# One hybrid layer stack on one core: own convolution taps ahead of the states, rotations one step later, the first memory layer in parts

## The chip, the cores and the metric

The kernel runs on one core of a Trainium2 chip. The metric is device time in microseconds (us) from the launch to the end on that core. The engines are named as in the profile: PE (TensorE, matmuls; PEld is its weight load), DVE (VectorE), ACT (ScalarE), POOL (GpSimd) and SP (SyncE, which issues most of the transfers). Each engine works through its own queue in order, and waits on semaphores for the others.

## The reference

The input x has 2 batches of 512 tokens with 512 channels, in float32. Six layers follow, each on a layer norm of x without weights:

```
x = x + 0.5 * ffn0(norm(x))      # int4 weights, 512 -> 1376 -> 512, silu(a) * b
x = x + ssm(norm(x))             # state-space layer, 128 heads of 64, 8 groups, state 128, chunks of 128
x = x + 0.5 * ffn0(norm(x))      # the same weights again
x = x + 0.5 * memory(norm(x))
x = x + attention(norm(x))       # 32 heads of 16, 8 key heads, rotary, causal
x = x + 0.5 * memory(norm(x))    # the same weights again
```

In the state-space layer a projection gives a gate, the rows hid, B and C, and dt. hid, B and C go through a causal convolution of four taps and a silu. Then each chunk has an inner part, (C B^T, times decays) times hid, and a part from the state that the chunks before it leave; the result is multiplied by silu(gate), normalised in groups of 1024 channels and projected back.

The memory layer computes, on a normed row h:

```
query  = h @ Wq.T                          # 64 wide
scores = (query @ Wr.T) @ (keys @ Wr.T).T / sqrt(48) + log_rel     # 128 slots
the 8 best slots by scores; weights w = softmax(query @ keys / 8 + log_rel) over them
out    = (w @ values) @ Wvd.T @ Wvu.T
u      = clip(0.5 * log1p(var h) / mean(log1p(var h)) + 2.5 * sigmoid(learned), 0, 5)
learned = gelu(h @ Wu1.T + bu1) @ Wu2.T
gate   = sigmoid(gate_w1 * clip((u - 0.5) / 1.5, 0, 1) + gate_bias), 0 below 0.05
return h + gate * out
```

The mean of log1p(var h) runs over all tokens of both batches.

## The kernel before

x stays on chip as eight tiles of 128 tokens by 512 channels (x[0] to x[7], batch b has the tiles 4b to 4b+3). `norm_parts` gives a norm in steps: `stats` (mean and variance, DVE), `root` (square root, ACT), `over` (reciprocal, DVE), `centre` (DVE; with a function `each` called on the normed tile) and `turn` (four transpositions on PE into a PSUM bank, hps, and a copy by ACT into hT). `start` is stats, root, reciprocal and centre in one.

Blocks written under `in_order` keep the order in which the code writes them on PE, DVE, ACT and POOL. Outside of them (memory setup, attention setup, nearly all of `memory`, and the second half of `end_last`) the framework's scheduler chooses the order: an instruction written earlier has priority, but one written later may go first when the earlier one isn't ready by its model. An `in_order` block's instructions may be interleaved with such free ones.

PSUM has eight banks, dealt out under names with a number of banks each; a matmul into a name waits until a bank of that name has been read. In the state-space stage they are tr 1, po 4, dd 1, mm 1, y 1; in the memory layers tr 2, mm 2, dd 2, y 2; in the attention pq 2 pairs, mx 2, av 1 and s 1.

The state-space stage is `period(n)`, n from 0 to 129: 128 steps (8 groups, in each both batches, in each 8 pairs of heads), and a pipeline in which step n is projected and convolved (`cur`), step n-1 (`p1`) makes its states and outputs, and step n-2 (`p2`) is projected back by `gather`. On PE a period has: the hid projection cp_h into dd (L881), a group's B or C projection into mm where it is due, the states st (L1074), the back projection po (L998), the outputs py in two halves (L1155, L1164), the gate projection pg into mm (L881), and transpositions of hid (L1208). On DVE it has, in order: hc, the gate's silu v (L904), two scans M (L972), the state recursion st (four operations, L1084), three own taps acc_h (`conv_taps`, L895), the taps of the B or C row, the products M with CB (L986), hid (L904), and yg (L1171, L1175). ACT has among others `first_tap` (acc, L890), the copy of the first state (L1079), the tanh th (L900), which closes `conv_taps`, and the exponentials of M.

`late` is the list of B and C rows of the group that comes next, each as three calls: `first` (first tap on ACT), `taps` (three taps on DVE, tanh on ACT) and `end` (silu on DVE). It holds one row in the sixth period of each eight (B) and in the seventh (C), and none in the others nor for the last group's second batch. Since cp_BT and cp_CT lie in mm, pg of the same period needs their taps to be done.

`memory` (L1255 on) is the first memory layer, written as one function for all tiles: norm, a second variance of each normed tile (`each`, L1264 to L1266), the mean of its logarithm (L1275 to L1285), then for each batch the gelu branch, the query, the route, scores and weights by tile (psc, sc, at, rest, top; L1338 to L1369), then one gate for all eight tiles (L1376 to L1400), and in an `in_order` block the additions to x with the attention's norm (L1410 to the end). The second memory layer is the class `Memory`, the same work in parts: `spread`, `learn`, `gelu`, `learned`, `query`, `route`, `score`, `weight`, `gate`, `add`. It takes the variance of the normed tile as variance times rstd times rstd, has one gate for each batch, and uses only the names dd, y and mm (and tr for turns). Its first batch is worked off within the attention, its second in `end_last`, after the attention.

In the attention, `attend` prepares batch 0 first and then runs 16 tiles (8 per batch) of four steps j. Each step has an `order` of maxima (mx), `weights` (PE: masks and scores w, L1774 and L1787; ACT: exponentials), `weigh` (av) and at j = 0 `normalise` (po in s); then come the `jobs` of that step; a tile ends with `turn_maxima` (pm in s, L1761; then mT on DVE). Batch 1's queries and keys are prepared by such jobs, in five units: `qk` in two halves (pqk in s; hi on ACT, lo and r on DVE, L1648 to L1672), `rotate` (prot in s, L1682; r on DVE; a POOL addition), `rotated` (rhi on ACT, rlo on POOL) and `spread_out` two or four times (pd in s, copied by ACT or DVE to q or k).

Of the kernel before, what the change touches and what calls it, by code (L numbers as in the profile page):

```python
# [10 lines left out]
F32 = mybir.dt.float32  # L11
# [7 lines left out]
P = 128  # L19
# [238 lines left out]
class Kernel:  # L258
# [135 lines left out]

    def norm(self, tag, each=None, gain=None):
        hT, start, turn = self.norm_parts(tag, each, gain)
        for t in range(NT):
            start(t)
            turn(t)
        return hT  # L400
# [602 lines left out]
    def period(self, n):  # L1003
# [29 lines left out]
        if cur is not None:  # L1033
# [21 lines left out]
            if n != 1:  # L1055
                conv = self.first_tap(p, cur.ct, f"h{cur.n}")
            if n == 0:
                th = self.conv_taps(*conv)
                self.group_bt(0, 0)
                self.turn(NT - 1, "po")  # L1060
                self.group_cb(0, 0, "po")
# [57 lines left out]
        if cur is not None:  # L1119
            if n > 0:  # L1120
                nc.scalar.activation(cur.M[1], cur.M[1], AF.Exp)
                self.setup_later(n, 1)
                th = self.conv_taps(*conv)
# [131 lines left out]
    def memory(self, n, then=None):  # L1255


        nc, m = self.nc, self.m
        with self.tc.tile_pool(name=f"mem{n}", bufs=1) as pool:
            mv2 = pool.tile([P, NT, 2], F32, name=f"mv2_{n}")  # L1260

            def each(t, h):
                st = pool.tile([P, 6], F32, tag="bn2", name=f"bn2_{n}{t}", bufs=3)
                nc.vector.bn_stats(out=st, in_=h)  # L1264
                nc.vector.bn_aggr(out=mv2[:, t, :], in_=st)
                nc.vector.scalar_tensor_tensor(  # L1266
                    out=self.x[t], in0=h, scalar=0.5, in1=self.x[t], op0=ALU.mult, op1=ALU.add
                )
                return h

            hT = self.norm(f"m{n}", each)


            lv = pool.tile([P, NT], F32, name=f"lv{n}")
            nc.scalar.activation(lv, mv2[:, :, 1], AF.Ln, bias=self.ones[:, 0:1])  # L1275
            tot = pool.tile([P, 1], F32, name=f"tot{n}")
            nc.vector.tensor_reduce(out=tot, in_=lv, axis=AX.X, op=ALU.add)
            pt = self.ps("tr", [P, 1], f"ptot{n}")
            nc.tensor.matmul(pt, lhsT=self.ones, rhs=tot, start=True, stop=True)
            nc.vector.tensor_scalar(  # L1280
                out=tot, in0=pt, scalar1=1.0 / (NB * S), scalar2=1e-6, op0=ALU.mult, op1=ALU.add
            )
            nc.vector.reciprocal(tot, tot)
            u = pool.tile([P, NT], F32, name=f"u{n}")
            nc.vector.tensor_scalar(  # L1285
                out=u, in0=lv, scalar1=tot, scalar2=0.5, op0=ALU.mult, op1=ALU.mult
            )

            sums = pool.tile([P, NT], F32, name=f"wsum{n}")
            learned = self.ps("y", [P, NT], f"learned{n}")  # L1290
            wT = []
            for b in range(NB):

                pz = self.ps("mm", [P, S], f"pz{n}_{b}")
                for k in range(KD):
                    nc.tensor.matmul(
                        pz, lhsT=m["m_wu1"][:, k, :], rhs=hT[b][:, k, :],
                        start=k == 0, stop=k == KD - 1,
                    )
                z = pool.tile([P, S], F32, tag="z", name=f"z{n}_{b}", bufs=2)  # L1300
                nc.scalar.activation(z, pz, AF.Identity, bias=m["m_cols"][:, 0:1])
                th = pool.tile([P, S], F32, tag="zt", name=f"zt{n}_{b}", bufs=2)
                nc.vector.tensor_tensor(out=th, in0=z, in1=z, op=ALU.mult)
                nc.vector.tensor_scalar(
                    out=th, in0=th, scalar1=0.044715, scalar2=1.0, op0=ALU.mult, op1=ALU.add
                )
                nc.vector.tensor_tensor(out=th, in0=th, in1=z, op=ALU.mult)
                nc.scalar.activation(th, th, AF.Tanh, scale=float(np.sqrt(2.0 / np.pi)))
                nc.vector.scalar_tensor_tensor(
                    out=th, in0=th, scalar=1.0, in1=z, op0=ALU.add, op1=ALU.mult  # L1310
                )
                for c in range(NC):
                    t = b * NC + c
                    nc.tensor.matmul(
                        learned[:, t : t + 1], lhsT=th[:, c * P : (c + 1) * P],
                        rhs=m["m_cols"][:, 1:2], start=True, stop=True,
                    )


                pq = self.ps("mm", [P, S], f"pq{n}_{b}")  # L1320
                for k in range(KD):
                    nc.tensor.matmul(
                        pq[:BOT], lhsT=m["m_wq"][:, k, :], rhs=hT[b][:, k, :],
                        start=k == 0, stop=k == KD - 1,
                    )
# [77 lines left out]
            with self.in_order():  # L1403
                if then is not None:
                    hT, _, turn = then()
                    stats, root, over, centre = self.norm_steps
# [610 lines left out]
```

## Time and profile before

| | us |
|---|---|
| median of 3 runs | 2785.98 |
| lowest and highest | 2782.41, 2788.01 |
| profiled execution, device time | 2794.43 |
| its span, first to last instruction | 2792.6 |
| PE busy | 2696.1 (97%) |
| DVE busy | 2029.1 (73%) |
| ACT busy | 1103.1 (40%) |
| POOL busy | 522.3 (19%) |
| first feed-forward layer, to about 283 | 283 |
| state-space stage, 283 to about 2125 | 1842 |
| second feed-forward layer, to about 2343 | 218 |
| first memory layer, to the first attention matmul at 2403.5 | 60.5 |
| attention, to about 2751 | 347.5 |
| rest of the second memory layer and the store | 41.6 |

The stage borders are read off the timeline. The mean granted clock of PE is 0.98 over the span: 1.00 in the state-space stage, 0.80 in the first memory layer, 0.93 and 0.90 in the attention's preparation and tiles, 0.74 in the last stretch. Durations of PE rows contain a modelled end, so neighbours overlap in the list by some 0.1 us. A float32 matmul shows as two passes of about 0.43 us for 512 columns at full clock.

### The profile page before, as it was taken

What the parts mean: (1) busy time and instruction counts of PE and PEld (TensorE: products, weight loads), DVE (VectorE), ACT (ScalarE), POOL (GpSimd) and SP (SyncE); (2) the same over time, 40 slices, a digit from 0 to 9 for tenths busy, and PEclk for the clock granted to TensorE, in tenths of its full rate; (3) what the DMA queues carried; (4) which work ended last, traced back from release to release, by engine and by line L of the source; (5) the groups of instructions that cost most, each with busy time, mean ns of one, the idle gap of its engine ahead of it and who ended that gap; (6) DMA issues with size and microseconds to landing.
All of it is one profiled execution on the core that took longest, in us unless ns stands there. A gap on an engine that the chain in (4) does not pass through costs nothing.

```text
span 2792.6 us, 33412 instructions
## 1 busy us (share of the span) xinstructions
PE 2696.1 (97%) x12208; PEld 1400.8 (50%) x12208; DVE 2029.1 (73%) x3627; ACT 1103.1 (40%) x2418; POOL 522.3 (19%) x344
## 2 busy tenths in 40 slices
PE   8999999999999999999999999999999999888997
PEld 3445555555555555555555555555555444445443
DVE  7846877888888788787787878878886443655555
ACT  2214443444444444344444434434443212344333
POOL 0001131323213222132322322223230000100000
PEclk9999999999999999999999999999999999889988
DMA  6623233223223323322322332232121010000000
GB/s 201 199 96 113 72 106 129 87 78 127 106 83 121 104 81 106 127 89 76 129 106 83 121 102 84 102 119 98 71 98 53 27 54 23 0 1 1 1 1 31
DMA packets 75620, 237.77 MB, mean 85 GB/s; under 512 B 9824, under 2 KB 10400, under 8 KB 58944
## 3 DMA queue, kind: packets, MB, share of 16 engines
q1 hardware_dynamic: 70416, 226.00, 23.6%
q10 hardware_dynamic: 4752, 8.65, 0.8%
q8 instruction: 97, 1.59, 0.2%
q0 software_dynamic: 288, 0.98, 0.1%
q14 instruction: 67, 0.55, 0.1%
HBM read 223.80 MB, written 11.80 MB: 84 GB/s over the span
## 4 chain that ended last, share of the span: by engine, by line
PE 84%; DVE 10%; ACT 4%; issue 1%; DMA 1%; POOL 0%; SPq 0%; ACTq 0%; DVEq 0%; POOLq 0%
PE pg L881 15%; PE po L998 14%; PE cp_h L881 14%; PE fo L667 5%; PE fmm L500 5%; PE py L1155 4%; PE st L1074 3%; PE fy L500 2%; DVE acc_h L895 2%; PE py L1164 2%; PE cp_BT L881 2%; PE cp_CT L881 2%; PE ht L1208 2%; PE w L1787 2%; PE fdd L500 1%
## 5 line engine op out<-in xcount | busy, mean ns | idle before, releaser
L881 PE MATMUL pg<-hT_s,wi 128*128 128x512 f32 x1024 | 472.5, 604 | 14.5 <-issue 6.9
L998 PE MATMUL po<-wo,yg 128*128 128x512 f32 x1024 | 460.7, 593 | 0.5 <-DVE yg L1175 0.5
L881 PE MATMUL cp_h<-hT_s,wi 128*128 128x512 f32 x1024 | 460.6, 592 | 0.0
L972 DVE TENSOR_TENSOR_SCAN M<-rows,later 128x512 f32<-128x512 f32 x256 | 458.4, 1829 | 0.0
L1182 POOL TENSOR_TENSOR ssum<-ssum,sq 128x512 f32<-128x512 f32 x112 | 142.3, 1270 | 1233.1 <-ACT sq L1181 1233.1
L881 PEld LDWEIGHTS pg<-hT_s,wi 128*128 128x128 f32 x1024 | 184.2, 189 | 221.7 <-issue 213.1
L895 DVE SCALAR_TENSOR_TENSOR acc_h<-cp_h,small,acc_h 128x511 f32<-128x511 f32 (+2 forms) x384 | 286.3, 745 | 9.0
L998 PEld LDWEIGHTS po<-wo,yg 128*128 128x128 f32 x1024 | 184.8, 190 | 184.4 <-issue 183.6
L881 PEld LDWEIGHTS cp_h<-hT_s,wi 128*128 128x128 f32 x1024 | 184.6, 190 | 183.6 <-issue 183.6
L988 POOL TENSOR_TENSOR Cs<-CT,rows 128x768 f32<-128x768 f32 x128 | 252.1, 1970 | 17.4 <-PE py L1164 15.7
L1084 DVE SCALAR_TENSOR_TENSOR st<-st,whole,st 128x64 f32<-128x64 f32 x512 | 108.8, 274 | 125.5 <-ACT st L1079 125.5
L900 ACT ACTIVATE th_h<-acc_h 128x512 f32<-128x512 f32 x128 | 80.5, 629 | 292.2 <-DVE acc_h L895 286.5
L1027 ACT ACTIVATE hd<-ht,end 128x64 f32<-128x64 f32 x768 | 171.1, 324 | 35.6 <-DVE hc L1019 35.5
L1181 ACT ACTIVATE sq<-yg 128x512 f32<-128x512 f32 x112 | 70.6, 630 | 287.1 <-DVE yg L1175 287.1
L986 DVE TENSOR_TENSOR M<-M,CB 128x512 f32<-128x512 f32 x256 | 164.6, 684 | 0.1
L977 ACT ACTIVATE M<-M 128x512 f32<-128x512 f32 x128 | 80.6, 630 | 199.1 <-DVE M L972 199.1
L1751 DVE CUSTOM_DVE_ANT_0 j<-s,future 128x384 f32<-128x384 f32 (+3 forms) x256 | 112.8, 487 | 53.4 <-PE s L1741 53.0
L1019 DVE TENSOR_TENSOR hc<-ht,dt 128x512 f32<-128x512 f32 x128 | 88.1, 689 | 85.6 <-PE ht L1208 85.6
L1155 PEld LDWEIGHTS py<-M,hc 128*64 128x64 f32 x2048 | 109.4, 136 | 68.2 <-issue 64.7
L1155 PE MATMUL py<-M,hc 128*64 128x128 f32 x2048 | 140.5, 279 | 1.1 <-DVE M L986 1.1
L1074 PEld LDWEIGHTS st<-hd,Btok 128*128 128x128 f32 x768 | 104.0, 191 | 70.2 <-issue 41.6
L904 DVE SCALAR_TENSOR_TENSOR v<-v,pg 128x512 f32<-128x512 f32 x128 | 87.5, 684 | 50.0 <-ACT v L1015 47.7
(386 smaller groups left out, 3780.7 us busy)
## 6 DMA issues: line engine op xcount, KB each, us to landing
rows<-rows SPq DMA_DIRECT2D x128, 1024.0 KB, 4.7
wi<-in_w_in_dram SPq DMA_DIRECT2D x144, 256.0 KB, 3.4
wo<-in_w_out_dram SPq DMA_DIRECT2D x64, 256.0 KB, 3.2
keep<-w ACTq DMA_DIRECT2D x33, 256.0 KB, 3.5
wk<-keep SPq DMA_DIRECT2D x33, 256.0 KB, 2.7
wi<-in_q_dram SPq DMA_DIRECT2D x44, 128.0 KB, 3.1
sc<-in_s_dram SPq DMA_DIRECT2D x44, 128.0 KB, 3.3
wi<-in_q_dram SPq DMA_DIRECT2D x11, 256.0 KB, 3.5
```

Of the source, the lines that this page charges most:

```text
L500: nc.tensor.matmul(dst, lhsT=w[:, k, :], rhs=x[:, k, :], start=start and k == 0, stop=stop and k == 1, skip_group_check=True,)
L667: nc.tensor.matmul(po, lhsT=act[ht][:, b, c * P : (c + 1) * P], rhs=w2[ht], start=ht == 0, stop=ht == NHT - 1,)
L881: self.nc.tensor.matmul(p, lhsT=wt[:, k, :], rhs=self.hT[b][:, k, :], start=k == 0, stop=k == KD - 1)
L895: self.nc.vector.scalar_tensor_tensor(out=acc[:, s:], in0=p[:, : S - s], scalar=w[:, 3 - s : 4 - s], in1=acc[:, s:], op0=ALU.mult, op1=ALU ...
L972: self.nc.vector.tensor_tensor_scan(out=m, data0=rows[:, i, 0, :], data1=self.later, initial=0.0, op0=ALU.add, op1=ALU.mult,)
L986: self.nc.vector.tensor_tensor(out=m, in0=m, in1=sh["CB"], op=ALU.mult)
L988: self.nc.gpsimd.tensor_tensor(out=cur.Cs, in0=sh["CT"][:, P:].unsqueeze(1).to_broadcast([P, 2, S - P]), in1=cur.rows[:, :, 1, P:], op=ALU ...
L998: self.nc.tensor.matmul(self.po[c], lhsT=p2.yg[:, c * P : (c + 1) * P], rhs=self.wo[p2.ct], start=p2.q == 0, stop=p2.q == PAIRS - 1,)
L1027: nc.scalar.mul(hd[:, c, ch], p1.pt[:, c, ch], self.dec["dt_end"][:, b * NC + c, h0 + i : h0 + i + 1],)
L1074: nc.tensor.matmul(pst[:, c, :], lhsT=self.sh[p1.g, p1.b]["Btok"][:, c, :], rhs=hd[:, c, :], start=True, stop=True,)
L1155: nc.tensor.matmul(py[ch, cs], lhsT=hc[:, c, ch], rhs=p1.M[i].rearrange("p (c t) -> p c t", c=NC)[:, c, :], start=c == 0, stop=c == 0, ski ...
L1182: nc.gpsimd.tensor_tensor(out=self.ssum, in0=self.ssum, in1=sq, op=ALU.add)
```

## The change

Four things are edited.

- `period`: where `late` is not empty, the own `conv_taps` (three taps on DVE, tanh on ACT) is written right after the own first tap, ahead of the states; in the other periods it stays where it was.
- `attend`: for each of batch 1's five units, `rotate` moves from step 3 of tile t to step 0 of tile t+1, `rotated` from step 0 to step 1, and each `spread_out` one step on.
- `memory`: the long function is replaced by an object of the class `Memory` with number 0. Its parts are called in the order learn, gelu, query, route, learned, then score and weight for each tile, then gate, batch by batch; the closing block is unchanged but for `m.add(t)`. So the second variance of each tile goes, the gate is made per batch, sc and rest have one buffer instead of two, and the bank names are those of `Memory`.
- `end_last`: for batch 1 of the second memory layer, query and route are written first, then learn, then the scores and weights, and gelu, learned and gate(0) after them.

The function `norm`, which only the old `memory` called, goes too.

```diff
@@ period
             if n != 1:
                 conv = self.first_tap(p, cur.ct, f"h{cur.n}")
+            if n == 0 or late:
+
+                th = self.conv_taps(*conv)
             if n == 0:
-                th = self.conv_taps(*conv)
                 self.group_bt(0, 0)
...
             if n > 0:
                 nc.scalar.activation(cur.M[1], cur.M[1], AF.Exp)
                 self.setup_later(n, 1)
-                th = self.conv_taps(*conv)
+                if not late:
+                    th = self.conv_taps(*conv)
             for one in late:
                 one[1]()
@@ memory
-    def memory(self, n, then=None):
...
+    def memory(self, then):
+        with self.tc.tile_pool(name="mem0", bufs=1) as pool:
+            m = Memory(
+                self, 0, pool, lambda tag, name: pool.tile([P, S], F32, tag=tag, name=name, bufs=2)
+            )
+            for t in range(NT):
+                m.start(t)
+                m.turn(t)
+            m.spread()
             for b in range(NB):
...
+                m.learn(b)
+                m.gelu(b)
+                m.query(b)
+                m.route(b)
+                m.learned(b)
                 for c in range(NC):
...
+                    m.score(b, c)
+                    m.weight(b, c)
+                m.gate(b)
             with self.in_order():
...
+                hT, _, turn = then()
+                stats, root, over, centre = self.norm_steps
                 for t in range(NT):
...
+                    m.add(t)
                     stats(t)
                     if t % NC == NC - 1:
                         root(t + 1 - NC, t + 1)
@@ end_last
         m.spread()
-        m.learn(1)
-        m.gelu(1)
         m.query(1)
         m.route(1)
-        m.learned(1)
-        m.gate(0)
+        m.learn(1)
         for c in range(NC):
             m.score(1, c)
             m.weight(1, c)
+        m.gelu(1)
+        m.learned(1)
+        m.gate(0)
@@ attend
             job(t, 1, self.qk, 1, u, 0)
             job(t, 2, self.qk, 1, u, 1)
-            job(t, 3, self.rotate, 1, u)
-            job(t + 1, 0, self.rotated, 1, u)
+            job(t + 1, 0, self.rotate, 1, u)
+            job(t + 1, 1, self.rotated, 1, u)
             for i in range(4 if u == 4 else 2):
-                n, j = divmod(4 * t + 5 + i, 4)
+                n, j = divmod(4 * t + 6 + i, 4)
                 job(n, j, self.spread_out, 1, u, i, "s")
```

## The prediction

> **What bounds the kernel now.** I read the page's head and clock row first, then the list of waits for the state-space stage, then the timeline where those waits fall, and last the timelines of the attention and memory stages.
>
> ```profile
> span 2792.6 us, 33412 instructions
> ...
> PE 2696.1 (97%) x12208; PEld 1400.8 (50%) x12208; DVE 2029.1 (73%) x3627; ACT 1103.1 (40%) x2418; POOL 522.3 (19%) x344
> ...
> PEclk9999999999999999999999999999999999889988
> ```
> ```profile
> PE pg L881 <- issue: 6.9, 14, 0.7
> PE pg L881 <- DVE acc_BT L895: 5.1, 7, 0.7
> PE pg L881 <- DVE acc_CT L895: 2.4, 7, 0.3
> ```
>
> TensorE is busy 97% of the span, so only what makes PE wait, or work at a lower clock, counts. The second fence is the whole of PE's notable waiting between 270 and 2125 us (the next entry is 1.6 us): 28 waits ahead of the gate projection pg, 14.4 us. They lie in the 30 "late" periods, in which a B or C row of the next group is convolved too. An ordinary period repeats every 13.29 us, a late one every 17.4 us (pg starts 437.52, 454.97, 472.40).
>
> ```profile
> 449.51 0.86 DVE L1084 SCALAR_TENSOR_TENSOR st<-st,whole,st 128x64 f32<-128x64 f32 x4 [4.11 <-ACT st L1079]
> ...
> 450.29 2.31 DVE L895 SCALAR_TENSOR_TENSOR acc_h<-cp_h,small,acc_h 128x511 f32<-128x511 f32 x3
> ...
> 452.51 2.31 DVE L895 SCALAR_TENSOR_TENSOR acc_BT<-cp_BT,small,acc_BT 128x511 f32<-128x511 f32 x3
> ...
> 454.97 3.67 PE L881 MATMUL pg<-hT_s,wi 128*128 128x512 f32 x8 [0.73 <-DVE acc_BT L895]
> ```
>
> This is the late B period in the timeline (start, duration, engine, line, output<-input, and in brackets the idle time and its releaser). VectorE (DVE) stands idle for 4.11 us until the state copy on ScalarE (ACT) frees st; only then come the own taps (acc_h) and the B taps (acc_BT), and pg, which needs the bank that acc_BT reads, starts 0.73 us late. In the C period the wait is 0.34 us.
>
> ```profile
> 2488.67 0.47 PE L1714 MATMUL pd<-rlo,spread 128*128 128x512 f32 x1 [0.47 <-DVE O L1824]
> ...
> 2500.55 0.47 PE L1682 MATMUL prot<-hi,spread 128*128 128x512 f32 x1 [0.81 <-DVE r L1672]
> ...
> 2502.04 0.66 PE L1761 MATMUL pm<-masks,top 128*128 128x128 f32 x4 [0.78 <-DVE r L1685]
> ...
> 2506.79 0.27 PE L1774 MATMUL w<-mask 128*128 128x128 bf16 x2 [0.64 <-ACT w L1793]
> ```
>
> In the attention stage the rotation matmul (prot) waits 0.81 us for the bank that VectorE still reads, and the transposition of maxima (pm) behind it 0.78 us. The first and last lines show what stands at a first step (j = 0): 0.47 us behind the normalisation, 0.64 us for the exponentials.
>
> ```profile
> 2388.59 0.75 DVE L1413 SCALAR_TENSOR_TENSOR x<-pmo,gate,x 128x512 f32<-128x512 f32 x1
> ...
> 2394.94 0.72 DVE L1413 SCALAR_TENSOR_TENSOR x<-pmo,gate,x 128x512 f32<-128x512 f32 x1
> ...
> 2403.46 1.02 PE L1659 MATMUL pqk<-hT_a,a_wqk 128*128 128x512 f32 x2
> ```
> ```profile
> 2774.52 0.28 DVE L189 SCALAR_TENSOR_TENSOR sc<-psc,m_rel 128x128 f32<-128x128 f32 x1
> ...
> 2784.28 1.41 DVE L253 SCALAR_TENSOR_TENSOR x<-pmo,gate,x 128x512 f32<-128x512 f32 x2
> ```
> ```profile
> 2343.00:2403.50 60.50, 50.01 (x168) 25.01 (x168) 40.26 (x130) 22.73 (x48) 0.00 (x0) 0.80 0.07 26
> ...
> 2360.00:2374.00 14.00, 14.00 (x38) 6.92 (x38) 6.09 (x31) 2.62 (x8) 0.00 (x0) 0.63 0.00 0
> ```
>
> The three fences above: first the end of the first memory layer, with the first addition to x, which needs the whole gate, at 2388.59, the fifth at 2394.94, the first attention matmul at 2403.46; then the kernel's end, from the first score row to the last additions; then, per stretch, length, busy time and count of PE, weight loads, DVE, ACT and POOL, and the granted clock: the layer takes 60.5 us at 0.80.
>
> **A, own taps ahead of the states.** Nothing is added; in 30 late periods three taps (2.31 us) and a tanh (0.63 us) move ahead of the state recursion. At 442 us the scans end by 445.40 (449.51 - 4.11) and the first tap on ACT at 445.84, so taps run to 448.2 and the tanh to 448.8, before the st copy is ready (449.22). Then st (0.86) and acc_BT end at 452.7 instead of 454.82; PE would come to pg at 454.24, so the 0.73 us goes, with 1.5 us to spare. In the C period the own tanh ends at 467.2, where the st copy ran at 466.65: the copy slips 0.6 us, st ends at 468.4, acc_CT at 470.7, and PE comes to pg at 472.06: 0.34 us goes, 1.3 us to spare. Behind the waiting tanh on ACT are the st copy, the B or C row's first tap and the second exponential; the next users are py's second half (at 471.2, st done 468.4) and times_c, both later. What is late next is nothing but PE. Sum: -14.4 us, from -12 (half of the C waits kept) to -15.4 (30 times the mean 0.51).
>
> **B, rotations one step later.** Five units. Each leaves step 3: prot's wait stays, since pm needs the same single bank (0.81), but prot's two passes (about 0.65, 2500.55 to the last pass) and pm's own wait (0.78) go: -1.43 x 5 = -7.2. At the next step 0, prot must wait until the normalisation is read (0.47) and takes 0.65, but the masks behind it wait 0.64 + 0.15 today: +0.3 in four units, +0.9 in the first, where no such wait stands: +2.1. The spreads end at step 3 now, so pm or the value projection waits for the q copy; such a wait is 0.7: three times, +2.1. The last k spread lands ahead of the first q projection in the same bank: +0.7. In the last unit two such waits move one step and remain. The rope multiply (0.69 on VectorE) falls where it is idle 0.72 for maxima; POOL's addition and subtraction (1.27 each) keep a whole step of 4 us. Sum -2.3; taken -2.2, from -5 (new waits covered by those for the exponentials) to +3 (all seven new waits and no cover).
>
> **C, first memory layer in parts.** Removed: 8 statistics rows (5.5 us for 8, 0.69 each) and 8 aggregates (0.17) on VectorE, replaced by two small multiplies (0.16). VectorE paces the last rows from 2346.15 on; the hT copies end at 2353.9 and would end near 2352: -1.9. With a gate for each batch, batch 0's gate depends on scores done by 2375.2, and VectorE waits for batch 1's queries until 2380.9. So four additions with their statistics (2388.59 to 2394.94) can lie there: -6.35. The attention's first norm still stands behind the fifth addition, which needs batch 1's gate, so its 8.5 us tail stays. Added: a second set of nine gate operations (about 0.2 each, 1.8 us, hidden in the same gap; +1.8 if not), one-buffer scores (1.83 us a block at the kernel's end against 1.65 here: +0.7 a batch), and a square root for batch 0 that can now fall between exponentials: two more table loads of 1.28 and 0.30, of which ACT's gaps hide about half, +1.3. Sum -6.3, from -11 (the second batch's queries come earlier too) to +5 (the rival below).
>
> A rule speaks against this last part. The trace's load is 1.28 us and the next activation follows within 0.01 us of it (2354.83 to 2356.12). The Trainium skill, page "ScalarE: Activation LUTs", section "What ACT_TABLE_LOAD costs", gives about 1283 ns plus a drain of about 1380 ns, 2.66 us for each switch. By that the two switches would cost 5.3 us in place of 2.6 and C would be near -5; the duration in the trace is used.
>
> **D, queries first at the end.** The query chain today starts behind pmz: pmq runs 2766.17 to 2769.8, scores start at 2774.52. Put first, pmq starts at 2760.76 in pmz's place at the same low clock; the route follows near 2768, and scores, behind pmz's rest on PE, start near 2771.5: -3. But gelu's four VectorE operations (0.69 + 0.43 + 0.69 + 0.69 = 2.5 us), which hide under the query chain today, now share VectorE with the scores, and two additions (0.75 each) made in its gaps today may follow: +2.5 to +4. Sum +0.5, from -2.5 (scores run ahead of pmz's rest) to +4 (gelu, its tanh and the gate wholly behind the scores).
>
> **Sum.** -14.4 - 2.2 - 6.3 + 0.5 = -22.4 us. The profiled execution took 2794.43 us (span 2792.6 and 1.8 around it), so 2772.0; it is 0.3% above the median of the runs, 2785.98, from which the forecast is 2763.6, say 2764.
>
> **Rivals.**
> 1. The memory layer gains nothing. Scores, transposed weights and projections now share two "dd" banks, so batch 1's projections hold the bank that batch 0's transposed weights need; PE is full between 2360 and 2374 at a clock of 0.63. Serial blocks, at most 3.6 us each (1.83, exponential 0.6, transposition and copy 0.7, hand-overs 0.5), make 29 us for eight against about 20 now, +9, and eat the -6.35. Then 2785.98 - 14.4 - 2.2 + 0.5 and up to +5: 2770 to 2775.
> 2. The wait ahead of pg only changes its releaser. If something else than the taps held that bank, A is worth 0: 2786 - 8 = 2778. For it, half of the waits (6.9 us) name no releaser; against it, they come at the same places and lengths (0.69, 0.30) with the taps ending just before.
> 3. Slower: the own tanh holds the st copy. On ACT's queue it now stands ahead of the st copy and of the next row's first tap. If the own taps start 2.2 us or more later than I place them, as with late scans, pg waits more than today. Each further microsecond costs 30. At 2.4 us pg would wait 1.15 instead of 0.48: +20 - 8 = +12, 2798. Against it: the scans show no wait for their rows.
> 4. More is gained: queries of batch 1 move up too and D gives its -2.5: near 2756.
>
> The granted clock is a fifth unknown, without a sign: the attention's first two tiles ran at 0.57 and 0.72, and the first took 20.4 us where later ones take 17.2, so one dip more or less is about 3 us. The Trainium skill, page "TensorE: Matmul & The Clock Gate", section "Part 1: The HAM clock gate", says that an idle window of about 3.4 us halves the clock. That agrees with 0.64 from 2389 to 2403, where PE waits 3.65 us; it gives no sign either.
>
> **How the numbers follow.** Likeliest 0.62; rival 1 0.17; rival 2 0.08; rival 3 0.07; rival 4 0.06. The likeliest's own range is 2756 to 2772; with the bounds of C and D and rivals 1, 2 and 4 it is 2751 to 2780. A measurement can tell about 0.2%, 5.6 us. The likeliest, rivals 1 and 4 and most of rival 2 are faster: 0.87; part of rival 2, 0.05, within; rival 3 and a poor sum of B, C and D, 0.08, slower.
>
> **What would show it.** A: no wait ahead of pg, late periods of 16.7 and 17.1 us, th_h ending before the B or C taps; else A is wrong. B: prot at step 0, pm in even tiles with one wait, not two. C: four additions to x before batch 1's scores end, the first attention matmul some 50 to 55 us after 2343, table loads between exponentials. D: scores starting before gelu's multiplies, and an end that moves less than 3 us. The prediction is wrong if pg still waits, or if the memory layer is as long as before.

## The result, and the profile after

The changed kernel takes 2763.39 us (median of four, 2761.28 to 2766.91), the kernel before 2786.02 us beside it (2782.41 to 2788.01). The ratio is 0.9918, with a 95% interval from 0.9891 to 0.9945: 22.8 us less, where 22.4 were forecast. The total is right; the terms of the sum are not. By the profiles, two gave more than forecast, one gave nothing, and one took a little.

The profiled execution of after took 2761.28 us (span 2759.5), that of before 2794.43 (span 2792.6). The head and the clock row of the page of after:

```profile
span 2759.5 us, 33377 instructions
...
PE 2680.9 (97%) x12208; PEld 1394.8 (51%) x12208; DVE 2000.5 (72%) x3622; ACT 1108.9 (40%) x2428; POOL 522.5 (19%) x344
...
PEclk9999999999999999999999999999999999889997
```

PE is as full as before; the last slices of the clock are a little higher. By stage, each length read between rows of PE's timeline:

| stage (us) | before | after | difference |
|---|---|---|---|
| start to the first pg | 250.9 | 249.1 | -1.8 |
| state-space stage and the feed-forward layer behind it | 2092.1 | 2072.9 | -19.2 |
| first memory layer (p_vd to the first pqk) | 60.5 | 61.4 | +0.9 |
| attention (first pqk to the first row of the last output projection, pao) | 343.5 | 327.5 | -16.0 |
| end (from there) | 45.7 | 48.6 | +2.9 |

Not all of the first two differences belongs to the change. The first pg starts at 248.4 to 250.9 us in the profiles of kernels without A, and the first period of the state-space stage takes 20.3 to 23.2 us with A and without it. From the second pg to p_vd it is 2069.7 us before and 2052.6 after, 17.1 us less.

**A.** The notable waits of PE between 270 and 2112 us, in the list of waits of after (total, times, longest us), begin:

```profile
PE st L1069 <- ACT hd L1020: 0.9, 2, 0.5
PE pd_whole L791 <- DVE CB L949: 0.8, 1, 0.8
```

No wait ahead of pg is left. The late B period in the timeline of after:

```profile
440.56 2.32 DVE L888 SCALAR_TENSOR_TENSOR acc_h<-cp_h,small,acc_h 128x511 f32<-128x511 f32 x3 [0.48 <-ACT acc_h L883]
442.97 0.63 ACT L893 ACTIVATE th_h<-acc_h 128x512 f32<-128x512 f32 x1 [2.44 <-DVE acc_h L888]
...
444.15 0.85 DVE L1079 SCALAR_TENSOR_TENSOR st<-st,whole,st 128x64 f32<-128x64 f32 x4 [1.27 <-ACT st L1074]
444.93 2.31 DVE L888 SCALAR_TENSOR_TENSOR acc_BT<-cp_BT,small,acc_BT 128x511 f32<-128x511 f32 x3
...
448.86 3.70 PE L874 MATMUL pg<-hT_s,wi 128*128 128x512 f32 x8
```

The own taps and their tanh (th_h) fill VectorE's gap, the states and the B taps follow, acc_BT ends at 447.24, 1.6 us ahead of pg (1.5 forecast), and pg has no bracket: it did not wait. The late periods are now 16.72 us (B) and 17.05 us (C), from 17.5 for B and 17.4 for C.

**B.** In the timeline of the attention stage after:

```profile
2476.47 0.66 PE L1618 MATMUL pm<-masks,top 128*128 128x128 f32 x4 [0.72 <-DVE r L1529]
...
2480.63 0.47 PE L1539 MATMUL prot<-hi,spread 128*128 128x512 f32 x1 [0.47 <-DVE O L1681]
...
2494.72 0.66 PE L1618 MATMUL pm<-masks,top 128*128 128x128 f32 x4 [0.68 <-ACT V L1583]
```

The rotation stands at a first step behind the normalisation (0.47), pm of an even tile (2476.47) has one wait in place of two, and the next pm (2494.72) waits for a copy: as forecast.

**C.** The additions to x on VectorE after, and the first attention matmul on PE, in the timeline:

```profile
2351.97 0.75 DVE L253 SCALAR_TENSOR_TENSOR x<-pmo,gate,x 128x512 f32<-128x512 f32 x1
2353.58 0.72 DVE L253 SCALAR_TENSOR_TENSOR x<-pmo,gate,x 128x512 f32<-128x512 f32 x1
2361.79 0.75 DVE L253 SCALAR_TENSOR_TENSOR x<-pmo,gate,x 128x512 f32<-128x512 f32 x1 [0.65 <-PE pmo L248]
2364.72 0.75 DVE L253 SCALAR_TENSOR_TENSOR x<-pmo,gate,x 128x512 f32<-128x512 f32 x1 [0.30 <-PE pmo L248]
2374.93 0.75 DVE L253 SCALAR_TENSOR_TENSOR x<-pmo,gate,x 128x512 f32<-128x512 f32 x1
...
2383.41 1.02 PE L1516 MATMUL pqk<-hT_a,a_wqk 128*128 128x512 f32 x2
```

Four additions did move ahead of the second batch's scores, and only the fifth stands behind them. The layer is no shorter all the same. Why can be read where it is cut at the first score, at the last transposed weight and at the attention's first transposition. The middle two pieces, as stretches (length, busy time and count of PE, weight loads, VectorE, ScalarE and POOL, granted clock, DMA share and rate), first before, then after:

```profile
2361.99:2388.17 26.18, 22.09 (x69) 10.71 (x68) 16.03 (x76) 7.36 (x23) 0.00 (x0) 0.76 0.00 0
2388.17:2397.40 9.23, 4.83 (x8) 1.63 (x8) 8.78 (x20) 2.17 (x3) 0.00 (x0) 0.68 0.00 0
```
```profile
2340.67:2374.47 33.80, 27.51 (x77) 12.41 (x76) 24.36 (x97) 12.04 (x34) 0.00 (x0) 0.71 0.00 0
2374.47:2377.33 2.86, 0.47 (x2) 0.18 (x2) 2.61 (x8) 0.27 (x1) 0.00 (x0) 0.50 0.00 0
```

Behind the last weight 6.37 us are gone (9.23 to 2.86; 6.35 forecast). Between the first score and the last weight 7.62 us came in. What came in between is on PE of after:

```profile
2351.58 0.47 PE L213 MATMUL pmw<-masks,at 128*128 128x128 f32 x1 [0.75 <-ACT at L203]
2351.84 5.27 PE L126 MATMUL pmz<-hT_m,m_wu 128*128 128x512 f32 x8
2357.04 3.65 PE L162 MATMUL pmq<-hT_m,m_wq 128*64 128x512 f32 x8
```

The second batch's projections (pmz, pmq) start only when the first batch's fourth transposed weight (pmw) is through. That is 29.8 us after p_vd, where before the first chunk of that projection stood just ahead of the first batch's scores, 17.8 us after p_vd, and the rest among them. ScalarE's two forecast table loads are there too:

```profile
2364.03 1.28 ACT L352 ACT_TABLE_LOAD   x1
2367.18 0.30 ACT L352 ACTIVATE rstd_a<-mv_a,eps 128x4 f32<-128x4 f32 x1 [1.86 <-DVE mv_a L349]
2368.12 1.28 ACT L203 ACT_TABLE_LOAD   x1 [0.64 <-DVE top L202]
```

Ahead of the first score a third load has moved: the one for the logarithm of the variances. It ran behind the last copy of hT before; now it runs between the first copy and the second, and PE waits for that copy. ScalarE's row of before, then the rows of ScalarE and PE after:

```profile
2354.83 1.28 ACT L1275 ACT_TABLE_LOAD   x1
```
```profile
2325.86 1.28 ACT L108 ACT_TABLE_LOAD   x1
...
2327.98 1.14 PE L381 MATMUL hps_m<-masks,h_m 128*128 128x128 f32 x8 [1.43 <-ACT hT_m L387]
```

**D.** The end in VectorE's timeline after:

```profile
2737.63 0.29 DVE L189 SCALAR_TENSOR_TENSOR sc<-psc,m_rel 128x128 f32<-128x128 f32 x1 [4.50 <-PE psc L183]
...
2738.23 0.67 DVE L136 TENSOR_TENSOR mt<-mz 128x512 f32<-128x512 f32 x1
...
2747.04 0.17 DVE L221 TENSOR_SCALAR gate<-gate 128x4 f32<-128x4 f32 x1 [2.52 <-ACT gate L156]
...
2755.71 0.75 DVE L253 SCALAR_TENSOR_TENSOR x<-pmo,gate,x 128x512 f32<-128x512 f32 x1 [0.95 <-PE pmo L248]
```

The scores start 21.9 us ahead of the end (18.1 before), and gelu's multiplies lie among them. Then VectorE stands for 2.52 us, with half a score block in hand, because a gate operation stands ahead in its order and waits for the learned gate's tanh.

### The profile page after: what moved, and what is told of

It reads as the page before. It is cut to its first block, busy times and chain, and to the rows that moved or that the text cites. A ratio compares the mean times of both kernels' runs of the same rounds, so it can differ in the third digit from the quotient of the medians.

```text
span 2759.5 us, 33377 instructions
## 1 busy us (share of the span) xinstructions
PE 2680.9 (97%) x12208; PEld 1394.8 (51%) x12208; DVE 2000.5 (72%) x3622; ACT 1108.9 (40%) x2428; POOL 522.5 (19%) x344
## 3 DMA queue, kind: packets, MB, share of 16 engines
q1 hardware_dynamic: 70416, 226.00, 23.9%
## 4 chain that ended last, share of the span: by engine, by line
PE 86%; DVE 8%; ACT 4%; issue 1%; POOL 0%; DMA 0%; SPq 0%; ACTq 0%; DVEq 0%; POOLq 0%
PE po L991 15%; PE pg L874 14%; PE cp_h L874 13%; PE fo L660 5%; PE fmm L493 5%; PE py L1151 4%; PE st L1069 3%; PE py L1160 3%; PE fy L493 2%; PE cp_CT L874 2%; PE cp_BT L874 2%; PE ht L1204 2%; DVE acc_h L888 1%; PE w L1644 1%; PE fdd L493 1%
## 5 line engine op out<-in xcount | busy, mean ns | idle before, releaser
L965 DVE TENSOR_TENSOR_SCAN M<-rows,later 128x512 f32<-128x512 f32 x256 | 431.2, 1723 | 0.0
L979 DVE TENSOR_TENSOR M<-M,CB 128x512 f32<-128x512 f32 x256 | 165.9, 684 | 12.5 <-ACT M L1116 12.3
```

Of the source, the lines that this page charges most:

```text
L965: self.nc.vector.tensor_tensor_scan(out=m, data0=rows[:, i, 0, :], data1=self.later, initial=0.0, op0=ALU.add, op1=ALU.mult,)
L979: self.nc.vector.tensor_tensor(out=m, in0=m, in1=sh["CB"], op=ALU.mult)
```

## The experiments

**The four parts alone, each on the kernel before.** The edits are the four pieces of the diff shown above; the third (the memory layer) is the changed kernel with the other three undone:

```diff
+            if n == 0 or late:
+                th = self.conv_taps(*conv)
             if n == 0:
-                th = self.conv_taps(*conv)
...
-                th = self.conv_taps(*conv)
+                if not late:
+                    th = self.conv_taps(*conv)
```


> Own taps ahead of the states alone, on the kernel before. Theory 1 (the late periods give what the trace of the changed kernel shows, 16.0 us in 28 of them and 1.5 in the first two): about 17 us faster, 2769, ratio 0.994, late periods of 16.7 and 17.05 us, no wait ahead of pg. Rival (part of the gain of the state-space stage comes from elsewhere, and the wait list's 14.4 is the true price): 2772. If it is within 0.2% of before, the taps are not the cause at all.


```diff
-            job(t, 3, self.rotate, 1, u)
-            job(t + 1, 0, self.rotated, 1, u)
+            job(t + 1, 0, self.rotate, 1, u)
+            job(t + 1, 1, self.rotated, 1, u)
```


> Rotations one step later alone. Theory 1 (the order gives 2 to 3 us, and the other 13 us that the profiled attention got shorter by are granted clock, which falls differently from run to run): 2783, from 2779 to 2786; its profile shows even tiles of 16.0 and odd ones of 13.7 us at full clock, and stretches of half clock somewhere in the tiles. Rival (the moved rotations take away waits that made the clock fall): 2771 to 2775, and no half clock in the tiles but at the first one.


```diff
-    def memory(self, n, then=None):
+    def memory(self, then):
...
+                m.gate(b)
```


> First memory layer in parts alone. Theory 1 (the second batch's projections wait for the two dd banks until the first batch's transposed weights are through, which eats the hidden additions): 2786 within 3, and the stretch from the last feed-forward matmul to the first attention matmul 60 to 62 us, as before. Rival (the layer is shorter by the 6 us that the sum gave, and something else in the changed kernel hid it): 2780, stretch of 54 to 55 us.


```diff
-        m.learn(1)
-        m.gelu(1)
         m.query(1)
         m.route(1)
-        m.learned(1)
-        m.gate(0)
+        m.learn(1)
```


> Queries first at the end alone. Theory 1 (gelu and two additions are moved out of the query chain's shadow, among the scores): 3 us slower, 2789, the end 48 to 49 us from the last attention projection instead of 45.6. Rival (the end in the changed kernel was only unlucky with the clock): within 1 us of before, 2785 to 2787.

| part alone | median us | ratio, 95% interval | difference | where in its profile |
|---|---|---|---|---|
| kernel before beside them | 2788.39 | | | |
| A | 2774.54 | 0.9952 [0.9933, 0.9971] | -13.4 | second pg to p_vd -17.1 |
| B | 2779.22 | 0.9968 [0.9955, 0.9981] | -8.9 | attention -13.4 |
| C | 2790.38 | 1.0014 [0.9994, 1.0035] | +3.9 | memory layer +0.7; attention's last two tiles -5.8 |
| D | 2794.48 | 1.0013 [0.9997, 1.0030] | +3.6 | end +0.9 |

The differences are the ratios taken of 2788.39 us. A and B carry the gain. C and D give none; whether they cost is within their intervals. The sum is -14.8 against -22.8 measured for all four together. Each interval is some 4 to 6 us to either side, so that the four are not shown to be worth more together than apart.

Against what was expected of them: A's profile has the late periods that were named and no wait ahead of pg; its difference in time (-8 to -19 us) fits the 17 us of its theory and the 14 of its rival. B's time is at the low end of its theory's range; its profile has the even and odd tiles of 16.0 and 13.7 us that the theory named, and full clock from tile 1 to tile 12, as its rival said. C did what its first theory says. D's stage is longer by 0.9 us where 3 or nothing was expected, which decides for neither.

**B is order and clock.** The tiles of the attention stage, from one pm to the next, in us:

| tile | 0 | 1 | 2 to 8 | 9 | 10 to 13 | 14 |
|---|---|---|---|---|---|---|
| before | 20.4 | 17.1 | 112.7 | 22.9 | 75.6 | 29.8 |
| B alone | 18.8 | 13.6 | 110.8 | 19.8 | 75.7 | 26.6 |
| after | 18.8 | 13.6 | 110.7 | 19.8 | 75.2 | 24.4 |

Tiles 2 to 8, all at full clock, give 1.9 us, near what the order was forecast to give. Tiles 0, 1 and 9 give 8.2 us more. The 1.6 us of tile 0 are order too: its granted clock is no higher after (0.73) than before (0.75), and the later even tiles with a unit lose as much at full clock (17.5 to 16.0). The 6.7 us of tiles 1 and 9 come with the clock, which goes from 0.70 and 0.78 to 1.00. (Tile 14 lies between 24.4 and 29.8 us over all profiles, with no relation to an edit.) Here are the stretches of 20 us in which the clock differs (60 to 80 and 190 to 210 us from the first attention matmul), first before, then after:

```profile
2463.50:2483.50 20.00, 18.32 (x150) 9.36 (x148) 10.97 (x39) 8.12 (x14) 2.54 (x2) 0.74 0.00 1
2593.50:2613.50 20.00, 17.35 (x131) 8.86 (x129) 10.27 (x37) 8.29 (x14) 2.54 (x2) 0.74 0.00 0
```
```profile
2443.40:2463.40 20.00, 17.38 (x185) 9.34 (x183) 13.47 (x47) 9.99 (x17) 2.56 (x2) 1.00 0.01 2
2573.40:2593.40 20.00, 17.48 (x144) 9.21 (x144) 10.69 (x40) 8.85 (x15) 2.56 (x2) 1.00 0.00 1
```

The granted clock (the third number from the right) is 0.74 before and 1.00 after, and so it is in the profiles of all kernels that leave the rotations in place (before, A, C, D alone) against all that move them, but for a dip of 3.4 us near 209 us in one of these (e7 below). To see whether a unit's own two waits set the dip behind it, one unit of the five was moved at a time.

```diff
+            d = t == 8
...
-            job(t, 3, self.rotate, 1, u)
-            job(t + 1, 0, self.rotated, 1, u)
+            at1 = divmod(4 * t + 3 + d, 4)
+            job(*at1, self.rotate, 1, u)
+            at2 = divmod(4 * t + 4 + d, 4)
+            job(*at2, self.rotated, 1, u)
...
-                n, j = divmod(4 * t + 5 + i, 4)
+                n, j = divmod(4 * t + 5 + d + i, 4)
```


> The kernel before with only the last of the five query/key units moved a step later (the unit of tile 8; the four others keep their place). Theory: the 17-us tile that holds a unit's two waits at step 3 (0.81 and 0.78 us) is what the half clock of the stretch behind it hangs on, tile by tile. Then tile 9 takes 19.8 us in place of 22.9 and the dip of the clock at 190 to 210 us from the first attention matmul is gone, while tiles 0 and 1 keep 20.4 and 17.1 us and the dip at 60 to 80 us. Rival (the clock answers to the whole move, or to chance): both dips stay, or both go.

> The kernel before with only the first of the five units moved a step later (the unit of tile 0). Theory, tile by tile: tile 1 takes 13.6 us in place of 17.1 and tile 0 18 to 19 in place of 20.4, the dip at 60 to 80 us is gone; tile 9 keeps 22.9 us and its dip at 190 to 210 us. Rival (the whole move, or chance): both dips stay, or both go.

Their times are 2778.66 and 2794.92 us, one each; most of that difference is another stage's, told below. With the last unit moved, tile 9 takes 19.8 us, tiles 0 and 1 keep 20.3 and 17.1; its two stretches:

```profile
2454.60:2474.60 20.00, 18.32 (x150) 9.37 (x148) 10.98 (x39) 8.12 (x14) 2.54 (x2) 0.74 0.01 1
2584.60:2604.60 20.00, 17.90 (x163) 9.38 (x160) 11.75 (x41) 8.89 (x16) 2.56 (x2) 1.00 0.00 1
```

That is the theory. With the first unit moved (`d = t == 0`), tile 1 takes 13.6 us and the first dip is gone, but tile 0 stays at 20.9, and the second dip, whose unit was left in place, is gone too (tile 9 at 19.7). A dip stands 55 us later instead (tile 12 at 21.6, was 18.0; the third row):

```profile
2467.00:2487.00 20.00, 17.74 (x183) 9.52 (x182) 13.72 (x51) 8.71 (x15) 2.55 (x2) 1.00 0.01 2
2597.00:2617.00 20.00, 16.95 (x139) 8.90 (x140) 10.25 (x38) 7.92 (x13) 2.55 (x2) 1.00 0.00 1
2657.00:2667.00 10.00, 9.82 (x67) 5.33 (x66) 5.87 (x18) 4.62 (x6) 0.00 (x0) 0.55 0.00 0
```

So the first dip follows its unit in every profile, and the second does not. The tile-by-tile theory holds for one unit and falls for the other. Nor are the two waits enough: in before the same pair, 0.81 and 0.78 us, ends tiles 0, 2, 4, 6 and 8, and only behind tiles 0 and 8 does the clock fall. This is the stretch of before behind the pair of tile 2, whose rows the prediction shows (2500.55 and 2502.04):

```profile
2503.50:2513.50 10.00, 9.11 (x89) 4.99 (x90) 7.06 (x31) 6.21 (x9) 1.28 (x1) 1.00 0.00 0
```

The traces show what tells the places apart. In all 14 of them the granted clock changes only between 0.50 and 1.00, and its changes lie whole multiples of 3.413 us apart. In before it falls at 2467.42, rises at 2477.66, falls at 2597.12 and rises at 2607.36: 3, 35 and 3 such periods. Extended over the attention, this grid cuts some of the pairs in two. Six profiles (before, A, C and D alone, the two with one unit moved) have 28 pairs. In nine, 1.46 to 1.60 us of the two waits lie in one period, and the clock is at 0.50 behind each. In the other nineteen the grid divides the pair, with at most 1.12 us of it in one period, and the clock stays at 1.00 behind each. The pair of tile 8 is whole in before and divided in e10, though its waits are the same. This is a pattern over 28 places, read from traces as they fell; no run moved the grid. Idle time in general is not sorted as cleanly: a period with 1.35 us, in tile 9, passes at full clock in five profiles and is followed by the short dip in e7.

**Why C gives nothing: the banks, and behind them VectorE and the table loads.** Rival 1 named them, so the transposed weights of the first memory layer were put into the "tr" banks, on the changed kernel (e5) and on the changed kernel with the old end (e6). The changed kernel itself (e8) and with the old end (e7) stand beside them.

```diff
-        pw = self.k.ps("dd", [P, P], f"pmw{n}_{b}_{c}")
+        pw = self.k.ps(self.turned, [P, P], f"pmw{n}_{b}_{c}")
...
+        self.wide, self.turned = ("dd", "dd") if n else ("dd", "tr")
```


> The changed kernel, the first memory layer's transposed weights in the bank name tr instead of dd. Theory 1 (sharing dd held the second batch's projections back until the first batch's weights were through): the second batch's pmz runs among the first batch's scores, the stretch from the last feed-forward matmul to the first attention matmul falls from 61.4 to about 55, and the time by 6 us. Rival (PE at half clock or the table loads hold the layer, not the banks): stretch 60 or more, no gain.

> Both: transposed weights in tr and the end as before. Theory 1: the two gains add, about 9 us faster than the changed kernel, 2755. Rival: no more than 3 us faster.

> The changed kernel with the end as before (learn, gelu, query, route, learned, gate(0), then scores). Theory 1 (queries first costs 3 us, the tail 48.6 against 45.7): 2760, tail 45 to 46. Rival (the 3 us are clock): within 1 us of the changed kernel, tail 48.

> The changed kernel once more, as the measure for the three others of this set. 2761 to 2767. If the attention's granted clock follows the order of the work, its tiles repeat those of the first profile: 18.8 and 13.6 for the first two, 19.8 for the tenth; if it is chance, they fall back to 20.4, 17.1 and 22.9.

| kernel | median us | ratio to before (2790.41) | memory layer us, its granted clock | end us |
|---|---|---|---|---|
| e8, changed kernel again | 2766.50 | 0.9909 [0.9885, 0.9933] | 60.2, 0.77 | 46.8 |
| e7, old end | 2764.40 | 0.9905 [0.9880, 0.9931] | 59.1, 0.83 | 45.6 |
| e5, weights in tr | 2763.54 | 0.9900 [0.9876, 0.9924] | 63.8, 0.79 | 46.4 |
| e6, weights in tr, old end | 2764.44 | 0.9904 [0.9880, 0.9928] | 62.0, 0.81 | 45.4 |

All four are the same within their intervals, and none of e5, e6 and e7 shows the 6, 9 and 3 us that their first theories named. Of the tiles that e8 was to repeat, tiles 1 and 9 do (13.6 and 19.8), and tile 0 does not (20.7 for 18.8). With the first unit moved, tile 0 takes 18.5 to 18.9 us in five profiles and 20.7 to 21.5 in four (e6, e8, e10, e12), where the half clock in it lasts 23.9 us instead of 17.1.

The banks do hold the projections back: with the weights in tr, the second batch's projection stands among the first batch's scores again, in PE's timeline of e5:

```profile
2348.64 0.63 PE L184 MATMUL psc<-m_keys,mq 64*128 64x128 f32 x2
2349.20 2.08 PE L127 MATMUL pmz<-hT_m,m_wu 128*128 128x512 f32 x2
2351.21 0.79 PE L183 MATMUL psc<-m_rk,mrq 48*128 48x128 f32 x2
```

But the layer does not get shorter for it. The second batch's scores then meet the additions of the first on VectorE, and the table loads on ScalarE; two stretches and ScalarE's timeline of e5:

```profile
2368.40:2379.30 10.90, 6.08 (x21) 2.63 (x20) 10.73 (x49) 3.59 (x10) 0.00 (x0) 0.93 0.00 1
2379.30:2381.70 2.40, 0.00 (x0) 0.00 (x0) 0.01 (x1) 2.32 (x6) 0.00 (x0) 0.50 0.00 0
```
```profile
2378.11 1.28 ACT L353 ACT_TABLE_LOAD   x1
2379.40 0.30 ACT L353 ACTIVATE rstd_a<-mv_a,eps 128x4 f32<-128x4 f32 x1
...
2379.87 1.28 ACT L204 ACT_TABLE_LOAD   x1
```

VectorE is busy for 10.73 of 10.90 us: additions, statistics and gate operations lie between the score rows. PE works for 6.08 us of it. Then PE and VectorE stand for 2.4 us while ScalarE works: two table loads, the square root, a copy and the exponential. The gap on VectorE into which the four additions were to fall is there where the second batch's queries come late (before, after); in e5, with early queries, it is gone.

Whether the loads alone matter was to be seen by issuing the square root behind the fifth addition.

```diff
-                    if t % NC == NC - 1:
-                        root(t + 1 - NC, t + 1)
+                    if t == NT - 1:
+                        root(NC, NT)
                     if t == NC:
+                        root(0, NC)
```


> The changed kernel with the old order at the end, the first memory layer's transposed weights in the tr banks, and the square root of the attention's first four norms issued after the fifth addition to x, so that no table load falls between the second batch's exponentials. Theory (with the banks free, the table loads are what holds the second batch): the stretch from the state-space stage's end to the first attention matmul falls from the 62.0 us of the same kernel with the root early by the 2.6 to 3.1 us that the transposition waited, to 59 or less, and the whole to about 2761. Rival (PE at half clock and VectorE's order hold the layer, the loads hide in them): the stretch stays at 61 to 63 us and the whole at 2763 to 2765.

It took 2763.62 us, ratio 0.9909 [0.9875, 0.9943], as its rival said; its stretch of 56.4 us is nearer the theory, but at a higher clock. It is no test: in its trace the square root still runs at 2371.09 us with its two loads, between the third exponential of the second batch and the fourth, because the order in which ScalarE's instructions are issued came out as it was. What the loads cost by themselves stays open. It shows e6's order a second time: the memory layer took these 56.4 us at a clock of 0.88, where e6 had 62.0 at 0.81.

**The two parts that gain, together.** The kernel before with A and B alone, the old memory layer and the old end:

> The kernel before with the own taps and the rotations moved alone; the memory layer and the end as before. Theory (these two carry the whole gain, and the other two give nothing or take a little): state-space stage 16.6 us and attention 10 to 16 us shorter, memory stretch 60 us, end 45.5 us; 2760 to 2764, ratio about 0.991, no worse than the whole change. Rival (the memory layer in parts and the end add a gain in company with the others): 2766 to 2770.

It takes 2755.17 us (six, 2753.66 to 2766.80), ratio 0.9885 [0.9858, 0.9912], beside 2790.99 for the kernel before and 2763.62 (2762.15 to 2767.09) for e11 on the same chip. The expectation, 2760 to 2764, was too high. The gain is -32 us with an interval from -25 to -40, where the two alone add up to -22.3; by their own intervals the two can't be told apart. It is the shortest median of all, and four of its six times (2753.66 to 2756.31) lie below every time of a kernel with A, B and C together. The whole change is no better than these two parts. Whether C and D cost something stays open. The ratios' intervals overlap by 0.2%, and run by run the time goes with the mean granted clock: the four short runs have 0.987, the other two 0.982 and 0.984 with 2766.80 and 2763.34 us, and at these two clocks the changed kernel took 2766.91 and 2761.28 us. That the old memory layer brings about the higher clock is not shown.

**The clock in the memory layer.** The memory layer of before stands unchanged in seven profiles. Three of them span the range: before, at 0.80 as the prediction shows it, and the two with one unit moved (e9, the last; e10, the first), from p_vd to the first pqk:

```profile
2339.53:2394.59 55.06, 45.34 (x167) 22.34 (x167) 40.00 (x130) 22.75 (x48) 0.00 (x0) 0.91 0.09 29
```
```profile
2341.35:2406.99 65.64, 56.43 (x168) 28.26 (x167) 40.69 (x131) 22.73 (x48) 0.00 (x0) 0.71 0.08 24
```

The same code takes 55.06, 60.52 or 65.64 us, with the granted clock at 0.91, 0.80 or 0.71, while VectorE's busy time stays within 0.7 us and ScalarE's within 0.1. That is 10.6 of the 16.3 us between e9 and e10, and e12's profiled execution (2766.80, its longest) is one with 65.6 us. A single profile therefore can't price a change of this layer. An estimate for equal clocks: between the three points of the old layer, 0.77, 0.78 and 0.83 give 62.2, 61.7 and 59.0. The layer in parts, with 60.2, 61.2 to 61.4 and 59.1, is 0 to 2 us shorter. With the weights in tr (0.79, 0.81, 0.88: old 61.1, 60.0, 56.5) it is 0 to 3 us longer. The estimate is good to about 1 us: B alone has the old layer at 0.83 with 59.9.

## Why the prediction was right, point by point

**A: right, and 3 us short.** Forecast -14.4. The waits are all gone, and the 28 late periods of the listed waits are 16.0 us shorter (0.75 to 0.80 a B period, 0.34 to 0.39 a C period). The first two late periods give 1.5 more: their waits stand ahead of other projections of the setup, the largest 1.63 us before and 0.31 after. It is the 1.6 us that the prediction calls "the next entry" and leaves out. The periods behind the late ones lose 0.4, and 17.1 us stay, with A alone as with all four. The term was summed from the waits ahead of pg alone; its own upper end (30 times the mean, -15.4) was nearer. Rivals 2 and 3 are out: pg has no new releaser, and the B taps end 1.6 us ahead of it.

**B: the order right, the clock wrong.** Tiles 2 to 8 show -1.9 and tile 0 -1.6. If tile 1 would give back 1 us at equal clock, as tiles 5 and 7 do (12.7 to 13.7), the order is worth -2.5, an estimate, for -2.2. The step that failed is the sentence that the granted clock is "a fifth unknown, without a sign". It named the attention's slow first tiles (0.57 and 0.72 there; 0.75 and 0.70 from pm to pm) and what a dip is worth (3 us), and then gave it no sign. Two dips lay behind pairs of waits of which B takes one away, and with them went 6.7 us in tiles 1 and 9. Three more such pairs cost no clock. Measured alone B is worth -8.9 us (-5.3 to -12.5), beyond its end of -5.

The Trainium skill, page "TensorE: Matmul & The Clock Gate", section "A second HAM failure mode: psum-queue depth-cycling", tells of a kernel whose PE idles briefly and often for banks, so that its clock swings. That agrees with the dips here: around tiles 0, 1 and 9 the longest listed waits are 0.8 us, far under the 3.4 us window of the rule that the prediction cited. Nor is the prediction's own example a whole window of idling: PE's wait of 3.65 us before 2397.40 begins at 2393.75, and the clock falls at 2395.74, 2.0 us into it.

**C: rival 1 in place of the forecast.** Two steps of it hold: the tail behind the last weight lost 6.37 us (6.35 forecast), and the table loads came. One step that failed is "four additions with their statistics can lie there". They do lie there, but the gap was taken from a kernel whose projections stood in other banks. Now the second batch's projections start 12 us later after p_vd, and the stretch of scores and weights grows by 7.6 us (about 6.4 at equal clock, where before's piece would be 27.4 at 0.71, between 26.18 at 0.76 and 29.65 at 0.62 in e10). Rival 1 had this mechanism, with +9; it got a chance of 0.17. Other banks bring no measured gain, as e5 shows. The other step that failed is the hT copies, "-1.9": from p_vd to the first score it is 19.05 before and 18.62 after. There the transpositions now wait 1.43 us for ScalarE's second copy, which stands behind the table load and the logarithm (1.28 and 0.30 us). With the variance taken by a product, the logarithm is ready sooner and its load went ahead of the copies, so the time won on VectorE is paid on ScalarE. The sum of C also counts "+0.7 a batch" for one batch of two. By the prediction's own sign ("if the memory layer is as long as before"), this part of it is wrong: the first attention matmul comes 61.4 us after p_vd, where 50 to 55 were named.

**D: right in sign.** Forecast +0.5, range to +4; its stage is 0.9 us longer alone, and 1.2 and 3.0 longer in the two profiles of the whole change (46.8 in e8, 48.6 in after) than with the old end (45.6 in e7). Scores started earlier as said, and the 2.52 us wait of the gate goes toward the bound named for +4, the gate behind the scores. Part of the difference is clock: the end ran at 0.67 to 0.72 in the four profiles with queries first and at 0.76 to 0.77 with the old end, but for C alone, whose old end took 46.1 us at 0.71. The times of e7 and e8 don't separate.

**The sum.** About -17 (by its stage; -13.4 by its times), -9, about 0 and +1 to +3 stand where -14.4, -2.2, -6.3 and +0.5 stood. That the total was hit is luck: a gain that was not forecast (the clock in the attention, about 7 us) took the place of one that did not come (the memory layer, 6 us). Rival 4 is out as well: e5 has the early queries and no gain from them. Only A, the order in B and the tail of C are evidence for the way of working.

## What to carry to other kernels

When a part of a stage is freed by an earlier start, ask whether the gap that it is to fill exists because something else is late, and whether it is still there once that comes early. Where PE is the bound, a wait that PE takes for a bank is worth more than its length if the granted clock sinks behind it, so lay the clock by stretch beside the list of waits before pricing either. Look at every place with the same waits: here two of five had the dip behind them. Compare a stage across kernels at equal clock, and judge by parts alone as well as together: here half of the change did all of the work.

## What the runs showed of the hardware

The granted clock of one and the same instruction sequence, the first memory layer of before, was 0.91, 0.80 and 0.71 in three profiles, with 55.06, 60.52 and 65.64 us. In the attention stage its dips came at the same place in four of four profiles with the rotations in place. All changes of the clock lay on a grid of 3.413 us in each trace. Half clock followed a pair of bank waits in nine of nine places with 1.46 us or more of the pair in one period of the grid, and in none of nineteen with 1.12 us or less. The Trainium skill, page "TensorE: Matmul & The Clock Gate", section "Part 1: The HAM clock gate", says that the window in which activity is counted runs freely and that transitions shift from run to run. The first of these findings agrees with it, in that the same code met the clock otherwise, and the grid fits such a window; what is counted in it no run here shows. Each table load took 1.28 us, and the next activation could follow at once (2379.40 behind 2378.11 + 1.28).
